# Affinities with the centroids as weights on four column groups, maxima of four heads at once before the first exponentials, and two batches' statistics ahead of step 0

## The chip, the cores and the metric

The kernel runs on 1 core of one Trainium2 chip. The metric is the device time of one execution in microseconds (us). The kernel before was run 5 times: median 2185.6 us, from 2184.82 to 2187.02.

## What is computed

Two layers over x, 8 batches of 512 tokens with 256 features; all data are float32. Cut to what matters here:

```python
xn = layernorm(x)
# layer 0: attention, 16 heads of 16 features, softmax over all 512 keys
out0 = softmax(q @ k.T) @ v
# layer 0: mixture of 8 experts, each token goes to the nearest centroid
aff = xn @ centroids.T                      # 4096 tokens x 8
assign = argmax(aff, axis=1)
alpha = sigmoid(aff[assign])
h = layernorm(xn, ln_g[e], ln_b[e]); ye = xn + relu(h @ w1[e].T + b1[e]) @ w2[e].T + b2[e]
x = x + out0 + alpha * ye + (1 - alpha) * xn
# layer 1: causal attention, a convolution over its output, causal attention again, and a low-rank feed-forward
```

## The kernel before, in words

**Tiles and stages.** Tokens of a batch lie on 128 partitions in 4 chunks (`NC`). A batch is normalised twice: `first_norm` (L546) makes xn on ACT (L236), which feeds attention and affinities, and on POOL the input h of the experts (L553), which is normalised with the second row of `rs`. `first_features` (L567) transposes xn on PE into xT (`to_features`, L245): the first half of the features is copied out of PSUM by DVE (L247), the second by ACT (L249). `affinities` (L573) multiplies a batch's xT, as weights of 128 columns, with the 8 centroids as the moving operand (L577: 4 chunks x 2 halves of the features; every float32 matmul shows as two records, so 16) and DVE copies the 128x32 result (L584).

**Attention of layer 0** is 32 jobs (8 batches x 4 groups of four heads) of 8 steps each. The loop in `run` goes through steps t = 0 to 268. Step t does two things: `scores` (L323) computes the score blocks of one block of 128 queries for two heads, and DVE reduces each to its row maximum (L340); `exps` (L372), 12 steps later (`LEAD`), computes scores again with the maxima as a shift, and ACT makes the exponentials (L399). `attend` (L412) multiplies with the values every second step, `l0_done` adds the result to acc (L843 to L851). So the first 12 steps have maxima only, and the last 12 have exponentials only. In each step four matmuls on four row groups of 32 rows, two of maxima and two of exponentials, are issued together; in the first 12 steps only two are. The maxima have three PSUM banks (`mx`). When a job's maxima are there, `shift` (step 8 of the next job plus 1) transposes them (L353), DVE copies them (mT, L358) and SP writes them into a row of q by four DMAs (L360).

**What fills the steps.** After the matmuls of a step, `Work.fill` issues pieces: those with due times (projections L272, values L282, shifts), and a stream. The stream begins with the list `FIRST`, one entry per step, whose letters stand for statistics of a batch (s, L219), closing a group's norms (c, L224 to L231: group a is batch 0, b batches 1 to 3, e batches 4 to 7), xn and h (n), transposes (f) and affinities (a). FIRST has 11 entries. Then `routing` takes the maximum over the experts and the one-hot matrix (L620 to L634), counts with two matmuls (L640, L641), makes ranks (L643 to L653) and places (L657 to L680), and scatters the 32 pieces of h into DRAM by POOL, one per step (L693). After the scatter the stream loads the first expert's weights (L708, POOL) and its tokens (hs, L715, SP), waits 5 steps, and computes 23 blocks of 256 tokens (L724, L746, L757 to L776), 2.05 units of cost per step. Then `second_norm` (L462 gathers, L477 residual, L219 statistics, L236 norm) handles the first four batches, one piece each third step.

**Order.** Every engine runs its instructions in the order in which the program issues them; PSUM banks are handed round in rings (`banks_first` until the routing, three for maxima and five for the rest; then `banks_alone`).

```python
for at, call in ((t, Job.scores), (t - lead, Job.exps)):
```

Of the kernel before, what the change touches and what calls it, by code (L numbers as in the profile page):

```python
# [9 lines left out]
F32 = mybir.dt.float32  # L10
# [3 lines left out]
ALU = mybir.AluOpType  # L14
# [5 lines left out]
P = 128  # L20
# [3 lines left out]
NC = S // P  # L24
# [3 lines left out]
PH = 32  # L28
NE = 8
# [23 lines left out]


FIRST = (
    "s1 s2", "s3 c1 n1 a0", "n2 f1 s4", "n3 f2 a1 s5", "f3 a2 s6", "s7 c2 n4 a3", "n5 f4", "n6 f5 a4", "n7 f6 a5",
    "f7 a6", "a7",
)


# [77 lines left out]
def block_kernel(ctx: ExitStack, tc: tile.TileContext, x, a0_wqk, a0_bqk, a0_wv, a0_bv, cent, experts,  # L138
                 a1_wqk, a1_bqk, a1_wv, a1_bv, conv_w, conv_b, out_w, out_b, u1, v1, f_b1, u2, v2, f_b2, out):
    nc = tc.nc  # L140
# [43 lines left out]
    def share_banks(**kinds):  # L184

        rings.update({k: list(v) for k, v in kinds.items()})

    def bank(kind="mm"):
        rings[kind].append(rings[kind].pop(0))
        return rings[kind][-1]  # L190


    def banks_first():
        share_banks(mx=banks[:3], mm=banks[3:])

    def banks_alone():
        share_banks(mx=banks[:3], sc=banks[3:6], av=banks[6:7], mm=banks[7:])
# [4 lines left out]
    class Norms:  # L202
# [4 lines left out]
        def __init__(self, pool, bs, nm, twice):  # L207
            self.bs, self.nm, self.twice = bs, nm, twice
            n = len(bs) * NC
            self.mv = pool.tile([P, n, 2], F32, name=f"mv{nm}", bufs=1)  # L210
            self.rs = pool.tile([P, 2 if twice else 1, n], F32, name=f"rs{nm}", bufs=1)
            self.rs1 = pool.tile([P, n], F32, name=f"rs1{nm}", bufs=1) if twice else None
            self.nm_t = pool.tile([P, n], F32, name=f"nm{nm}", bufs=1)

        def stats(self, i):
# [6 lines left out]
        def close(self):  # L222
            rs = self.rs
            nc.vector.tensor_scalar(rs[:, 0, :], self.mv[:, :, 1], EPS, None, ALU.add)  # L224
            if self.twice:
                nc.vector.tensor_scalar(rs[:, 1, :], self.mv[:, :, 1], 1.0 + EPS, EPS * EPS, ALU.mult, ALU.add)
            nc.scalar.activation(rs, rs, AF.Sqrt)
            nc.vector.reciprocal(rs, rs)
            if self.twice:
                nc.vector.tensor_scalar(self.rs1, rs[:, 0, :], 1.0, None, ALU.add)  # L230
            nc.vector.scalar_tensor_tensor(self.nm_t, self.mv[:, :, 0], -1.0, rs[:, 0, :], ALU.mult, ALU.mult)  # L231

# [5 lines left out]
                    scale=self.rs[:, 0, n : n + 1],  # L238
                )

    def to_features(src, dst, off, k, nm):

        ps = bank()
        for c in range(NC):
            nc.tensor.transpose(ps[:, c * P : (c + 1) * P], src[:, c, k * P : (k + 1) * P], ident)  # L245
        if k == 0:
            nc.vector.tensor_copy(dst[:, k, off : off + S], ps)  # L247
        else:
            nc.scalar.copy(dst[:, k, off : off + S], ps)  # L249
# [170 lines left out]
    def run(jobs, work_of, layer, per_step, most):  # L420
        steps, lead, av_at = STEPS[layer], LEAD[layer], AV_AT[layer]
        last = max(av_at)

        def attend(t):
            for i, blocks in av_at.items():
                j, r = divmod(t - lead - i, steps)
                if r == 0 and 0 <= j < len(jobs):
                    for kc in blocks:
                        jobs[j].attend(kc, kc == 0, i == last and kc == blocks[-1])
                    if i == last:  # L430
                        jobs[j].done(jobs[j], t)

        work_of.first()
        for t in range(steps * len(jobs) + lead + last - steps + 1):
            work_of.t = t
            mm, after = [], []
            for at, call in ((t, Job.scores), (t - lead, Job.exps)):
                j, i = divmod(at, steps)
                if 0 <= j < len(jobs):
                    m, a = call(jobs[j], i)  # L440
                    mm.append(m)
                    after.append(a)
            for together in zip(*mm):
# [79 lines left out]
    with ExitStack() as l0:  # L523
# [7 lines left out]
        nc.scalar.dma_start(out=wv0, in_=a0_wv)  # L531
        bv0 = w0.tile([P, D], F32, name="bv0")
        nc.scalar.dma_start(out=bv0, in_=a0_bv)
        cent_sb = w0.tile([P, 2, NE], F32, name="cent_sb")
        nc.scalar.dma_start(out=cent_sb, in_=cent)

        later = ExitStack()
        pre = later.enter_context(tc.tile_pool(name="pre", bufs=1))
# [7 lines left out]
        def first_norm(norms, i):  # L546
            b = norms.bs[i]
            xn = work.tile([P, NC, D], F32, tag="o", name=f"xn{b}")
            norms.norm(i, xn)
            h = pre.tile([P, NC, D], F32, tag="h0", name=f"h0_{b}", bufs=NB)  # L550
            for c in range(NC):
                n = i * NC + c
                nc.gpsimd.tensor_scalar(  # L553
                    h[:, c, :], acc[b][:, c, :], norms.mv[:, n, 0:1], norms.rs[:, 1, n : n + 1],
                    ALU.subtract, ALU.mult,
                )
                firsts0[b, c] = norms, n
            h0.append(h)
            return xn
# [7 lines left out]
        def first_features(b, xn):  # L567
            t = big.tile([P, 2, S], F32, tag="xT", name=f"xT{b}")
            for k in range(2):
                to_features(xn, t, 0, k, f"a{b}")  # L570
            xT.append(t)

        def affinities(b):  # L573
            ps = bank()
            for c in range(NC):
                for k in range(2):
                    nc.tensor.matmul(  # L577
                        ps[:, c * NE : (c + 1) * NE],
                        lhsT=xT[b][:, k, c * P : (c + 1) * P],
                        rhs=cent_sb[:, k, :],  # L580
                        start=(k == 0),
                        stop=(k == 1),
                    )
            nc.vector.tensor_copy(  # L584
                aff[:, b * NC : (b + 1) * NC, :].rearrange("p c e -> p (c e)"), ps[:, : NC * NE]
            )

        def pt(shape, name, tag=None, bufs=1):
# [192 lines left out]

        def stream():

            norms = [first_norms] + [Norms(pre, bs, nm, True) for bs, nm in (((1, 2, 3), "b"), ((4, 5, 6, 7), "e"))]
            of = {b: (n, i) for n in norms for i, b in enumerate(n.bs)}
            xns = {}

            def stats(b):
                of[b][0].stats(of[b][1])

            def norm(b):
                xns[b] = first_norm(*of[b])

            def features(b):
                first_features(b, xns.pop(b))

            def close(i):
                norms[i].close()

            do = {"s": stats, "c": close, "n": norm, "f": features, "a": affinities}  # L800
            for t, pieces in enumerate(FIRST):
                for p in pieces.split():
                    do[p[0]](int(p[1]))
                if t == 1:
                    for n in range(NBLK):
                        nc.sync.dma_start(out=hs_z[n], in_=zeros)
                yield At(t + 1)
            banks_alone()
            yield from routing()
            later.close()  # L810
            moe = later.enter_context(tc.tile_pool(name="moe", bufs=2, reuse_waits="tile"))
            load_ffn()
            nc.sync.dma_start(out=ob_sb, in_=out_b)
            fb2_sb = work.tile([P, D], F32, tag="og", name="fb2_sb")
            nc.sync.dma_start(out=fb2_sb, in_=f_b2)
            nc.gpsimd.tensor_tensor(ob_sb, ob_sb, fb2_sb, ALU.add)
            nxt = Block(moe, 0)
            yield At(todo.t + 5)
            banks_experts()
            nxt.features()  # L820
            yield 0.5
            for n in range(NBLK):
                blk = nxt
                for f2 in range(NFC // 2):
                    blk.hidden(f2)
                    yield 1.75
                    if f2 == 0 and n + 1 < NBLK:
                        nxt = Block(moe, n + 1)
                if n + 1 < NBLK:
                    nxt.features()  # L830
                    yield 0.5
                for j in range(TB // P):
                    blk.output(j)
                    yield 3.5
            banks_alone()
            yield from second_norm(range(NB - N_LATE), "c", lambda n: At(todo.t + n))
# [47 lines left out]
            todo.add(t0 + STEPS[0] + 1, t0 + STEPS[0] + 1, 0.2, job.shift)  # L884

        banks_first()
        first_norms = Norms(pre, (0,), "a", True)
        first_norms.stats(0)
        first_norms.close()
        first_features(0, first_norm(first_norms, 0))  # L890
        todo.stream = stream()
        run(jobs, todo, 0, MOE_PER_STEP, 99)
        later.close()
# [323 lines left out]
```

## Time and profile before

| what | us |
|---|---|
| median of 5 runs | 2185.6 |
| the profiled execution, its own time | 2185.78 |
| its span, first to last instruction | 2184.0 |
| PE busy | 2075.6 (95%) |
| DVE busy | 1236.1 (57%) |
| ACT busy | 863.4 (40%) |
| POOL busy | 195.6 (9%) |
| mean granted clock of PE | 0.953 |

The page gives shares of the whole span. The work of one stage is read from the windows (busy time of each engine and the clock that was granted to PE, 1.00 being full speed, in a stretch of the span), from the groups of instructions (count, busy us, mean ns of one, idle time before them and what ended it), and from the timeline of an engine (start, duration, line, operation, count, idle time before it and its releaser). Times are counted from the first instruction.

### The profile page before, as it was taken

The numbers are of one execution on the slowest core, as the hardware profiler recorded it, in microseconds if no ns is written. First come the engines' busy times: TensorE is split into PE (matmuls) and PEld (weight loads), VectorE is DVE, ScalarE is ACT, GpSimd is POOL, SyncE is SP. The second block draws the span as 40 slices with busy tenths as digits, with TensorE's granted clock in tenths as the row PEclk, the third lists the DMA queues.
The fourth block names the chain that finished last, engine by engine and source line by source line (L and its number), as shares of the span: only waits on it lengthen the run. The fifth ranks groups of instructions, "written<-read, shape, count | busy, mean of one in ns | idle before, by whom it ended". The sixth has DMA issues, their size and how long they took to land.

```text
span 2184.0 us, 35488 instructions
## 1 busy us (share of the span) xinstructions
PE 2075.6 (95%) x13664; PEld 1050.1 (48%) x13664; DVE 1236.1 (57%) x3569; ACT 863.4 (40%) x1674; POOL 195.6 (9%) x222
## 2 busy tenths in 40 slices
PE   7997999999999999996798999999999999999998
PEld 4522555555555555542133455554554555554554
DVE  5465454555555554555322566676666666666662
ACT  2243333333333333334353244444444444444443
POOL 4355000000000000003320000000000000000000
PEclk7599999999999999996699799999999999999999
DMA  5013212221221212201100000000000000000000
GB/s 205 1 42 126 78 61 102 93 102 66 88 102 52 102 62 101 93 16 51 58 0 1 1 2 2 2 2 11 2 12 2 12 2 12 2 12 2 12 2 20
DMA packets 37064, 93.53 MB, mean 43 GB/s; under 512 B 5792, under 2 KB 27936, under 8 KB 33952
## 3 DMA queue, kind: packets, MB, share of 16 engines
q0 software_dynamic: 6384, 59.78, 7.4%
q1 hardware_dynamic: 29792, 30.56, 4.3%
q8 instruction: 107, 1.75, 0.3%
q10 hardware_dynamic: 720, 0.93, 0.1%
q14 instruction: 61, 0.50, 0.1%
HBM read 70.03 MB, written 20.45 MB: 41 GB/s over the span
## 4 chain that ended last, share of the span: by engine, by line
PE 80%; DVE 5%; issue 3%; ACT 1%; POOL 1%; another core or an unknown queue 0%; DMA 0%; DVEq 0%; POOLq 0%; ACTq 0%
PE bank L323 26%; PE bank L412 12%; PE bank L746 8%; PE bank L767 8%; PE bank L272 4%; PE bank L1023 4%; PE bank L390 4%; PE bank L372 3%; PE bank L282 2%; PE bank L1041 2%; PE bank L927 1%; PE bank L1075 1%; PE bank L940 1%; DVE jk L343 1%; PE bank L245 1%
## 5 line engine op out<-in xcount | busy, mean ns | idle before, releaser
L399 ACT ACTIVATE e<-bank 128x512 f32<-128x512 f32 (+1 forms) x1280 | 640.3, 552 | 968.8 <-PE bank L372 494.5
L323 PE MATMUL bank<-k,q 32*128 32x512 f32 (+3 forms) x3072 | 777.4, 538 | 30.0 <-DVE m L340 25.2
L372 PE MATMUL bank<-q,k 32*128 32x512 f32 (+3 forms) x3072 | 706.2, 538 | 12.8 <-DMA q<-mT 11.0
L343 DVE CUSTOM_DVE_ANT_0 jk<-bank,cmask 128x512 bf16<-128x512 f32 (+3 forms) x1024 | 502.9, 491 | 241.7 <-PE bank L323 162.7
L323 PEld LDWEIGHTS bank<-k,q 32*128 32x128 f32 x3072 | 303.9, 187 | 394.0 <-issue 167.3
L340 DVE TENSOR_REDUCE m<-bank 128x1 f32<-128x512 f32 x512 | 329.3, 685 | 165.1 <-PE bank L372 122.2
L412 PE MATMUL bank<-e,v 128*32 128x512 f32 (+3 forms) x3072 | 324.0, 509 | 0.7 <-ACT e L399 0.7
L372 PEld LDWEIGHTS bank<-q,k 32*128 32x128 f32 x3072 | 272.6, 187 | 36.7 <-issue 23.9
L746 PE MATMUL bank<-hsT,w 128*128 128x256 f32 x736 | 182.0, 393 | 0.7 <-ACT e L399 0.7
L746 PEld LDWEIGHTS bank<-hsT,w 128*128 128x128 f32 x736 | 135.4, 192 | 70.8 <-issue 53.3
L767 PE MATMUL bank<-w,hT 128*128 128x256 f32 x736 | 169.0, 383 | 0.0
L767 PEld LDWEIGHTS bank<-w,hT 128*128 128x128 f32 x736 | 136.1, 190 | 35.6 <-issue 19.0
L412 PEld LDWEIGHTS bank<-e,v 128*32 128x32 f32 x3072 | 68.0, 109 | 145.4 <-issue 138.3
L390 PE MATMUL bank<-mask_t,ident_bf 128*128 128x128 bf16 (+1 forms) x768 | 124.1, 244 | 0.0
L390 PEld LDWEIGHTS <-ident_bf 128*128 128x128 bf16 x768 | 43.6, 97 | 157.7 <-issue 142.5
L759 DVE TENSOR_SCALAR hT<-bank,w 128x256 f32<-128x256 f32 x92 | 44.5, 484 | 114.0 <-ACT hT L757 114.0
L1023 PE MATMUL bank<-ctxT,cw_sb 128*128 128x256 f32 x384 | 90.0, 383 | 2.1 <-DVE q L262 1.8
L343 DVE DVE_READ_ACCUMULATOR2_ANT m<- 128x1 f32 x1024 | 85.0, 83 | 0.4
L851 POOL TENSOR_TENSOR acc<-acc,og 128x256 f32<-128x256 f32 x32 | 23.2, 725 | 626.2 <-DVE og L847 626.2
L264 ACT ACTIVATE k<-bank,bqk,rows 128x512 f32<-128x512 f32 x64 | 46.3, 774 | 81.8 <-PE bank L272 71.7
L776 DVE TENSOR_TENSOR f<-bank,w 128x256 f32<-128x256 f32 x46 | 19.6, 425 | 102.1 <-PE bank L767 102.1
L1023 PEld LDWEIGHTS bank<-ctxT,cw_sb 128*128 128x128 f32 x384 | 70.1, 189 | 13.3 <-DVE q L262 3.2
(180 smaller groups left out, 1477.1 us busy)
## 6 DMA issues: line engine op xcount, KB each, us to landing
q<-mT SPq DMA_DIRECT2D x384, 2.0 KB
hs_d<-zeros SPq DMA_DIRECT2D x23, 256.0 KB
hs<-hs_d SPq DMA_DIRECT2D x23, 256.0 KB
fs_d<-f SPq DMA_DIRECT2D x23, 256.0 KB
acc<-in_x SPq DMA_DIRECT2D x8, 512.0 KB
out<-acc SPq DMA_DIRECT2D x8, 512.0 KB
cw_sb<-in_conv_w SPq DMA_DIRECT2D x1, 768.0 KB
wqk<-in_a_wqk ACTq DMA_DIRECT2D x1, 512.0 KB
```

The costliest lines, as they stand in the source:

```text
L264: nc.scalar.activation(dst, ps, AF.Identity, bias=bias[:, half : half + 1], scale=rows[:, half : half + 1])
L272: nc.tensor.matmul(ps, lhsT=w[:, k, col : col + P], rhs=src[:, k, :], start=(k == 0), stop=(k == 1))
L323: lambda h=h, qc=qc, at=at, nk=nk: nc.tensor.matmul(heads[h % 2][:, at : at + nk], lhsT=self.q[h * PH : (h + 1) * PH, qc * P : (qc + 1) * ...
L340: nc.vector.tensor_reduce(self.m[:, qc, h, :], src, AX.X, ALU.max, negate=True)
L343: nc.vector.tensor_tensor_reduce(out=junk[:, :nk], in0=src, in1=cmask[:, S - nk :], scale=1.0, scalar=-3e38, op0=ALU.add, op1=ALU.max, acc ...
L372: lambda h=h, kc=kc, at=at, lo=lo: nc.tensor.matmul(heads[h % 2][:, at : at + S - lo], lhsT=self.k[h * PH : (h + 1) * PH, kc * P : (kc + 1 ...
L390: nc.tensor.matmul(heads[h][:, : len(blocks) * P], lhsT=ident_bf, rhs=mask_t[:, : len(blocks) * P], start=False, stop=True,)
L399: nc.scalar.activation(e[:, h, :], heads[h][:, :n], AF.Exp, scale=self.scale)
L412: nc.tensor.matmul(self.av[h * PH : (h + 1) * PH, lo:], lhsT=self.v[:, kc, 4 * self.g + h, :], rhs=es[h // 2][:, h % 2, :], start=first, s ...
L746: nc.tensor.matmul(ps[:, i * TB : (i + 1) * TB], lhsT=w[:, O_W1 + k * FF + fc * P : O_W1 + k * FF + (fc + 1) * P], rhs=self.hsT[:, k, :], ...
L767: nc.tensor.matmul(ps[:, 0:D], lhsT=self.hT[:, fc, j * P : (j + 1) * P], rhs=w[:, O_W2 + fc * D : O_W2 + (fc + 1) * D], start=(fc == 0), s ...
L1023: nc.tensor.matmul(ps[:, :w], lhsT=cw_sb[:, k, tap, c * P : (c + 1) * P], rhs=ctxT[b % 2][:, k, tap + lo : tap + lo + w], start=(k == 0 an ...
```

## The change

- `cent_sb` is padded with zeros from 8 to 32 columns (a memset on DVE, and the DMA into the first 8). `affinities` loads the centroids as weights and streams xT; the four chunks go to four column groups of 32. The 128x128 result (expert by token) is copied by ACT (affT), transposed on PE, and DVE copies the 32 wanted columns into aff.
- In layer 0, steps below 12 do the maxima of two steps in each even step and none in odd ones, with four PSUM banks; the bank rings change at step 12.
- FIRST has 8 entries instead of 11; the statistics of batches 1 and 2 are issued ahead of step 0. Routing is issued from step 8 on instead of step 11, and so is all that follows it in the stream.
- Both halves of xT are copied by ACT.
- POOL's h is a multiplication and an addition instead of a subtraction and a multiplication; DVE makes the extra operand nm2 at each close.

```diff
-    "s1 s2", "s3 c1 n1 a0", "n2 f1 s4", "n3 f2 a1 s5", "f3 a2 s6", "s7 c2 n4 a3", "n5 f4", "n6 f5 a4", "n7 f6 a5",
-    "f7 a6", "a7",
+    "s3 c1 n1 a0", "n2 f1 s4 s5", "n3 f2 a1 s6 s7 c2", "f3 a2 n4", "f4 a3 n5", "f5 a4 n6", "f6 a5 n7",
+    "f7 a6 a7",
...
-        share_banks(mx=banks[:3], mm=banks[3:])
+        share_banks(mx=banks[:4], mm=banks[4:])
...
+                nc.vector.scalar_tensor_tensor(self.nm2, self.mv[:, :, 0], -1.0, rs[:, 1, :], ALU.mult, ALU.mult)
...
-        if k == 0:
+        if k == 0 and eng is None:
...
+            if layer == 0 and t == lead:
+                banks_alone()
+            if t >= lead or layer == 1:
+                maxima = (t,)
+            else:
+                maxima = (t, t + 1) if t % 2 == 0 else ()
-            for at, call in ((t, Job.scores), (t - lead, Job.exps)):
+            for at, call in [(i, Job.scores) for i in maxima] + [(t - lead, Job.exps)]:
...
-        cent_sb = w0.tile([P, 2, NE], F32, name="cent_sb")
-        nc.scalar.dma_start(out=cent_sb, in_=cent)
+        cent_sb = w0.tile([P, 2, PH], F32, name="cent_sb")
+        nc.vector.memset(cent_sb, 0.0)
+        nc.scalar.dma_start(out=cent_sb[:, :, :NE], in_=cent)
...
-                    h[:, c, :], acc[b][:, c, :], norms.mv[:, n, 0:1], norms.rs[:, 1, n : n + 1],
-                    ALU.subtract, ALU.mult,
+                    h[:, c, :], acc[b][:, c, :], norms.rs[:, 1, n : n + 1], norms.nm2[:, n : n + 1],
+                    ALU.mult, ALU.add,
...
-            for c in range(NC):
-                for k in range(2):
+            for k in range(2):
+                for c in range(NC):
                     nc.tensor.matmul(
-                        ps[:, c * NE : (c + 1) * NE],
-                        lhsT=xT[b][:, k, c * P : (c + 1) * P],
-                        rhs=cent_sb[:, k, :],
+                        ps[c * PH : (c + 1) * PH, 0:P],
+                        lhsT=cent_sb[:, k, :],
+                        rhs=xT[b][:, k, c * P : (c + 1) * P],
...
+            affT = pre.tile([P, P], F32, tag="affT", name=f"affT{b}", bufs=2)
+            nc.scalar.copy(affT, ps[:, 0:P])
+            ps = bank()
+            nc.tensor.transpose(ps[:, 0:P], affT, ident)
             nc.vector.tensor_copy(
-                aff[:, b * NC : (b + 1) * NC, :].rearrange("p c e -> p (c e)"), ps[:, : NC * NE]
+                aff[:, b * NC : (b + 1) * NC, :], ps[:, 0:P].rearrange("p (c e) -> p c e", e=PH)[:, :, :NE]
             )
...
-            banks_alone()
             yield from routing()
...
-        first_norms.stats(0)
-        first_norms.close()
-        first_features(0, first_norm(first_norms, 0))
+        norms[0].stats(0)
+        norms[0].close()
+        first_features(0, first_norm(norms[0], 0))
+        for i in range(2):
+            norms[1].stats(i)
```

More of the change, by code (lines that the diff above doesn't have):

```diff
@@ L212, in __init__ @@
             self.rs1 = pool.tile([P, n], F32, name=f"rs1{nm}", bufs=1) if twice else None
+            self.nm2 = pool.tile([P, n], F32, name=f"nn{nm}", bufs=1) if twice else None
             self.nm_t = pool.tile([P, n], F32, name=f"nm{nm}", bufs=1)
@@ L239, in norm, with to_features @@
                 )
-    def to_features(src, dst, off, k, nm):
+    def to_features(src, dst, off, k, nm, eng=None):
         ps = bank()
@@ L569, in first_features @@
             for k in range(2):
-                to_features(xn, t, 0, k, f"a{b}")
+                to_features(xn, t, 0, k, f"a{b}", "s")
             xT.append(t)
@@ L782, in stream @@
         def stream():
-            norms = [first_norms] + [Norms(pre, bs, nm, True) for bs, nm in (((1, 2, 3), "b"), ((4, 5, 6, 7), "e"))]
             of = {b: (n, i) for n in norms for i, b in enumerate(n.bs)}
@@ L886, in block_kernel @@
         banks_first()
-        first_norms = Norms(pre, (0,), "a", True)
-        first_norms.stats(0)
-        first_norms.close()
-        first_features(0, first_norm(first_norms, 0))
+        norms = [Norms(pre, bs, nm, True) for bs, nm in (((0,), "a"), ((1, 2, 3), "b"), ((4, 5, 6, 7), "e"))]
+        norms[0].stats(0)
[3 more added lines that the diff above has]
+            norms[1].stats(i)
         todo.stream = stream()
```

## The prediction, made before the changed kernel was run

> **What bounds the kernel now.** PE is busy for 95% of the span, but that is a mean over stages, and the change edits only the first one. So I read the busy time and granted clock by window, then the groups and timelines of 0 to 225 us, and last the end of layer 0. Columns of the window line: stretch, length, busy us of PE, PEld, DVE, ACT, POOL, granted clock, DMA share, GB/s.
>
> ```profile
> 57.00:89.00 32.00, 31.84 (x119) 22.87 (x117) 9.88 (x19) 9.89 (x20) 18.70 (x16) 0.50 0.00 1
> ```
>
> Here PE has no gap, at half clock, and the others are mostly idle: PE is the bound. In order of time (start, us):
>
> ```profile
> 62.07 1.97 PE L245 MATMUL bank<-ident,xn 128*128 128x128 f32 x8
> 63.83 3.42 PE L577 MATMUL bank<-cent_sb,xT 128*128 128x8 f32 x16
> 67.18 2.08 PE L323 MATMUL bank<-k,q 32*128 32x512 f32 x4
> 69.19 1.97 PE L245 MATMUL bank<-ident,xn 128*128 128x128 f32 x8
> ```
>
> A step takes 7.1 us: transposes, one affinity of 16 matmuls that stream 8 columns each after a 128-column weight load (3.42 for almost no work), and one pair of maxima (2.08).
>
> The routing at the end of this stage releases the scatter of 32 pieces on POOL, and that releases the experts. First and last scatter, then the first expert weights (POOL); then what PE does meanwhile:
>
> ```profile
> 113.92 1.21 POOL L693 DMA_INDIRECT hs_d<-h,pos_i  x1 [38.22 <-issue]
> ...
> 205.28 1.02 POOL L693 DMA_INDIRECT hs_d<-h,pos_i  x1 [1.09 <-DMA hs_d<-h,pos_i]
> 206.35 0.55 POOL L565 TENSOR_SCALAR acc<-acc,rs1e,nme 128x256 f32<-128x256 f32 x1
> 206.88 0.71 POOL L816 TENSOR_TENSOR ob_sb<-ob_sb,fb_sb 128x256 f32<-128x256 f32 x1
> 208.58 1.00 POOL L708 DMA_INDIRECT w<-in_experts,wrow_i  x1 [0.99 <-DMA hs_d<-h,pos_i]
> ```
>
> ```profile
> 203.91 2.05 PE L323 MATMUL bank<-k,q 32*128 32x512 f32 x4
> 216.92 2.08 PE L372 MATMUL bank<-q,k 32*128 32x512 f32 x4 [10.96 <-DMA q<-mT]
> 218.93 1.11 PE L724 MATMUL bank<-ident,hs 128*128 128x128 f32 x4
> 220.73 8.09 PE L746 MATMUL bank<-hsT,w 128*128 128x256 f32 x24 [0.69 <-ACT e L399]
> ```
>
> Each scatter waits for the one before (91.4 us for 31 intervals, 2.95 each), and PE has run out of steps at 206: from here to 221 the scatter, not PE, sets the time. **So the gain is read at the first scatter (113.92), not from PE's saved work.** From 221 to 975 PE is busy 98 to 100%; nothing there is edited.
>
> **The change, worked out as a chain to the first scatter.** (Rows on the left are of before; L numbers are its own.)
>
> 1. Start. The memset of cent_sb and the new nm2 are two small DVE operations, some 0.1 each (small ones start 0.08 to 0.1 apart): +0.2. The cent_sb DMA now waits for that memset at about 6.6 (3.0 before), and ACT's table load (1.28) and first square root stand behind it: load done at about 8.5, square root due at 9.2, so hidden by 0.7. It lands in 32-byte pieces, but its first reader comes at 21. xT's first half by ACT (0.59) instead of DVE (0.69): nothing. First maxima at 20.3 (20.11).
> 2. Statistics of batches 1 and 2 (8 x 0.53 = 4.2) go to DVE's idle 9.9 to 17.0: hidden if x has landed; at 340 to 400 GB/s batch 2 (2.5 MB in all with the weights) lands by 9.5. Four maxima on four row groups: the later rows have four such matmuls in 1.1 (0.70 + 0.59, overlapped), so 21.4. Four reductions 2.5, statistics of batch 3 2.1, close 1.25: 27.3. Before, the first xn of batch 1 started at 31.31: 4.0 gained.
> 3. xn 2.07, then the first affT copy, for which PE waits, having nothing else in its order (128x128 on ACT: between 0.23 of a 128x32 and 0.59 of a 128x512 copy, I take 0.3): 29.75. Affinity transpose 0.25, transposes of xn 1.97: 32.0.
> 4. PE: maxima 2.1, xn2 2.0, affinity 1, ACT's copy and its wait 0.4, transpose 0.25: 37.75. DVE: statistics 4 and 5 after aff0 (30.2), four reductions, aff1 at 37.8, statistics 6 and 7 4.2, close 1.3: 43.5. Before, 56.5.
> 5. From 45.7 on ACT paces batches 4 to 7: xn 2.07, PE's transposes after its last piece 1.0, xT copy 0.6, affT 0.3, handovers 0.2: 4.2 each (7.1 before), to 62.5. The six maxima of steps 4 and 6 and most affinities lie beside xn. Last two affinities: 64.5.
> 6. Four maxima 2.1, reductions 2.5 after the first: 68. Maximum to one-hot took 94.33 to 100.19; 3.0 of that was a wait for ACT, which stood in k (1.45) and the table load (1.28); now ACT is idle: 2.9, so 71. The two count matmuls 2.0, cum to rank 3.35, four reductions 2.5, q 1.5 (its projection, 5.65, is ready by 79), place and pos_i 3.65: 84.1. POOL answers in 0.9: **first scatter at 85.0, 28.9 earlier.**
>
> The affinity itself: 8 matmuls of 512 columns on four column groups (L412) take 1.06 at full clock, so 16 of 128 columns 0.53, at half clock 1.06; upper end 3.42, the old price, if loads still rule. I take 1.06, as L412 has this tiling; on the path lie some 0.5 of it. POOL's h falls from 1.22 to 0.55 each (the row of L565, mult and add); POOL has 30 us to spare, so nothing.
>
> The clock: I keep 0.50 from 30 us on, as 57 to 89 shows that gapless PE alone didn't raise it. If it is 1.0, chain items of PE halve, some 8 us less.
>
> [...]
>
> **Scatter to experts.** 36 steps of PE (92 us for 37 before) and 91.4 of scatter still run side by side. Before, PE then waited for q<-mT, queued on SP behind hs, which waits for the last scatter. The experts now start in step 49, not 52; its exps need no new q, so PE waits for hs itself, ahead of q<-mT on SP. Worth between 0 and 3 (the 2.08 of L372 and part of the queue): 1.5.
>
> **What is given back.** Everything from routing on runs three steps earlier in a loop of 269 steps, so the experts end at step 243, not 246, and three more steps follow them. The last steps have exponentials only, at half clock:
>
> ```profile
> 1045.43 2.08 PE L372 MATMUL bank<-q,k 32*128 32x512 f32 x6
> 1048.19 2.07 PE L372 MATMUL bank<-q,k 32*128 32x512 f32 x2 [0.67 <-ACT e L399]
> 1050.18 1.94 PE L412 MATMUL bank<-e,v 128*32 128x512 f32 x8
> 1052.05 2.08 PE L372 MATMUL bank<-q,k 32*128 32x512 f32 x6
> ```
>
> Five took 1045.4 to 1061.4, 3.2 each: three more, +9.6 (5.8 at the 1.93 of 1014 to 1018). And the last residual and statistics group (L477, L219; 1016.6) now has maxima of three steps before it on DVE, 3 x 1.2 less the mT copy: +3.4 (0 if hidden). Together +13.0, bounds 5.8 to 14.
>
> **Sum**, against the profiled execution of 2185.8 (span 2184.0, 1.8 around it; the runs' median is 2185.6): 2185.8 - 28.9 - 1.5 + 13.0 = **2168.4**.
>
> **Rivals.**
> - *The stall at 989 goes.* In the chain that ended last there is
>
> ```profile
> 989.14 7.15 another core or an unknown queue
> ```
>
> with DVE and ACT both idle amid POOL's gathers. Nothing in the program asks for it; with other instructions beside the gathers it may not recur: 2168.4 - 7.2 = 2161.
> - *The scatter paces longer.* Its first intervals were 3.4, not 2.95, while the clock was half. If 3.45 held for 31 intervals: + 15.5 = 2183.9, no change. Against: it fell to 2.72 soon after.
> - *The affinities don't get cheaper.* 2.36 more each, 8 times: + 18.9 = 2187.3, no change. Against: L412.
> - *Slower: the new round trip PE, ACT, PE.* If each affT copy stood behind ACT's xn (2.07) and two copies (1.1), PE would wait 3.2 each, 8 times: + 25.6 = 2194. It decides from 2.15 us each (17.2 / 8). For: the first one does wait so. Against: each later copy is issued after the xT copies and ahead of the next xn, when PE has just finished.
>
> **How the numbers follow.** Chances: forecast 0.64 (own range 2160 to 2178, from the bounds of clock, tail and experts), stall gone 0.20, scatter 0.05, affinities 0.04, slower 0.07. Faster by over 0.2% (4.4 us, about what a measurement of this kernel can tell) is 0.64 + 0.20 = 0.84; within 0.09; slower 0.07. The range goes from 2152 (stall gone and PE at full clock) to 2182, which takes in the bounds of the tail and half of the scatter case.
>
> **What would show it.** First xn of batch 1 at 27 (step 2); close of batches 4 to 7 at 43.5; L577's successor at 0.5 to 1.1 per 16; first scatter at 85; last one 91 later; first L746 at about 190; five exponential-only steps become eight at 3.2. Wrong would be: PE idle for 2 us or more before each affinity transpose, a scatter pace above 3, or experts that start late though the scatter ended early.

## The result: no difference, and the profile after

The changed kernel's runs have a median of 2186.1 us (44 runs, 2163.9 to 2201.5), the kernel before beside them 2184.5 us (86 runs). The ratio of changed to before is 0.9994, with a 95% interval from 0.9982 to 1.0005: no change, where 2168.4 was forecast. (The ratio leaves out runs over 1.5% above the fastest of their kernel, so it lies below the ratio of the two medians.) The profiled execution took 2180.98 us (span 2179.2, mean granted clock 0.962). In the lines of after, L325, L374, L414 and L761 are the L323, L372, L412 and L746 of before, L588 is the affinity, L598 the transpose behind it, L708 the scatter and L342 the maxima's reduction.

The start went as forecast. The window 57 to 89 of the kernel after, with the columns shown before:

```profile
57.00:89.00 32.00, 21.39 (x106) 8.68 (x104) 22.00 (x62) 9.73 (x20) 3.34 (x4) 0.74 0.02 8
```

PE is busy for 21 of 32 us in place of 31.8, and at 0.74 of full clock in place of 0.50. In order of time, on PE:

```profile
52.73 0.64 PE L588 MATMUL bank<-xT,cent_sb 128*32 128x128 f32 x16
53.81 0.33 PE L598 MATMUL bank<-ident,affT 128*128 128x128 f32 x1 [0.44 <-ACT affT L596]
54.07 1.14 PE L325 MATMUL bank<-k,q 32*128 32x512 f32 x8
```

An affinity costs 0.64 here, at full clock (1.00), and 1.08 where e1 (the same kernel profiled again) ran it at half clock; before it cost 1.85 at full clock (from 42.0 on, at 1.00) and 3.42 at half (from 46.3 and from 63.8 on, at 0.50). Its round trip through ACT costs 0.39 to 0.44 of waiting, but for the first, which waits 7.61 for a copy that stands behind the first xn on ACT. First and last scatter (POOL), then the experts' start (PE):

```profile
83.70 1.21 POOL L708 DMA_INDIRECT hs_d<-h,pos_i  x1 [31.91 <-issue]
...
175.15 1.02 POOL L708 DMA_INDIRECT hs_d<-h,pos_i  x1 [1.10 <-DMA hs_d<-h,pos_i]
```

```profile
180.48 1.09 PE L739 MATMUL bank<-ident,hs 128*128 128x128 f32 x4 [5.35 <-DMA hs<-hs_d]
187.85 4.37 PE L761 MATMUL bank<-hsT,w 128*128 128x256 f32 x10 [6.28 <-DVE hsT L744]
```

The first scatter is 30.2 us earlier, the first expert matmul 32.9. The end of the span is 4.8 us earlier. So 28 us were lost behind the experts' start. The lengths of all stages, in us (landmarks read from the timelines of POOL and PE; the experts' stretch goes from the start of their first matmul to the end of the last; e1, e2, e5 and e15 are experiments below):

| stage | before | after | e2: before again | e1: after again | e5: experts in step 52 | e15 |
|---|---|---|---|---|---|---|
| to the first scatter | 113.9 | 83.7 | 112.5 | 87.0 | 89.1 | 89.2 |
| to the last scatter | 91.4 | 91.4 | 93.9 | 94.6 | 92.5 | 93.0 |
| to the first expert matmul | 15.4 | 12.7 | 15.6 | 12.9 | 15.6 | 17.2 |
| the experts' stretch | 754.6 | 767.9 | 754.7 | 765.7 | 754.8 | 752.1 |
| to the feed-forward (end of layer 0) | 88.5 | 88.9 | 68.3 | 83.2 | 80.6 | 71.7 |
| to the first maxima of layer 1 | 131.2 | 132.1 | 130.9 | 130.3 | 131.6 | 131.2 |
| to the last output projection ahead of the final pair (L1075, L1090 of after) | 941.5 | 942.3 | 937.4 | 943.8 | 937.4 | 941.3 |
| to the end | 47.5 | 60.2 | 55.4 | 55.3 | 55.6 | 53.1 |

Before and after as first profiled differ, from top to bottom and before rounding, by -30.2, +0.1, -2.7, **+13.3**, +0.4, +0.8, +0.8 and **+12.7**: the sum is -4.8. Two rows take the gain back. They are of different kinds, as the columns of e1 and e2 show: the experts' stretch repeats, the last row does not.

**The experts' stretch.** Its window, of before and then of after:

```profile
220.73:975.28 754.55, 744.69 (x4100) 399.75 (x4100) 395.42 (x715) 270.53 (x502) 38.27 (x46) 1.00 0.22 79
```

```profile
187.85:955.75 767.90, 750.60 (x4092) 403.44 (x4096) 394.83 (x712) 269.71 (x502) 37.45 (x45) 1.00 0.22 79
```

The same instructions, but for a few at the edges, at the same full clock: PE is idle for 17.3 us in place of 9.9 (length less busy time) and 5.9 busier. What PE waited for in it (us in total, times, longest), of before and of after:

```profile
PE bank L323 <- DVE m L340: 9.9, 12, 1.2
```

```profile
PE bank L325 <- DVE m L342: 17.3, 24, 1.2
```

Twice as many waits for the maxima. One of them in detail, in e1, on PE and then on DVE:

```profile
246.32 0.59 PE L325 MATMUL bank<-k,q 32*128 32x512 f32 x2
246.34 0.59 PE L374 MATMUL bank<-q,k 32*128 32x512 f32 x2
248.11 1.29 PE L325 MATMUL bank<-k,q 32*128 32x512 f32 x3 [1.18 <-DVE m L342]
248.72 0.70 PE L374 MATMUL bank<-q,k 32*128 32x512 f32 x2
```

```profile
245.93 0.72 DVE L856 STREAM_TRANSPOSE avt<-bank 128x512 f32<-128x512 f32 x1 [0.60 <-PE bank L414]
...
247.03 0.42 DVE L860 TENSOR_TENSOR og<-avt,rec 128x256 f32<-128x256 f32 x1
247.38 1.28 DVE L342 TENSOR_REDUCE m<-bank 128x1 f32<-128x512 f32 x2
```

PE ended a step's scores at 246.9. That step, of odd number, got no piece of the stream, and the values' matmuls (L414, 1.07), which come in even steps, had been the step before; so the next step's maxima are due at once. While the experts run, the maxima have two PSUM banks (`banks_experts`; the three named ahead of the prediction hold outside the steps of the experts), both filled by the step before, and DVE, held up by a finished job's output (L856 to L860), empties the first only at 248.1. PE loses 1.18 us waiting, and some 0.6 more because the maxima now start alone and the exponentials' scores follow instead of running beside them: 248.11 to 249.84, 1.73 for what takes 1.13 (245.79 to 246.93). That second part stands in the profile as busy time. By the totals, 12 more waits cost 7.4 idle and 5.9 busy. Nearly all of the busy part lies in the two score matmuls. Their busy time together, of before and then of after (columns here: PE, PEld, DVE):

```profile
220.73:975.28 754.55, 236.45 (x1548) 69.97 (x1548) 18.36 (x24) 1.00 0.22 79
```

```profile
187.85:955.75 767.90, 241.77 (x1544) 72.47 (x1544) 18.35 (x24) 1.00 0.22 79
```

That is 5.3 of the 5.9.

**The tail.** The exponential-only steps that had run at half clock in before (2.08 for four L372 records, at 0.50), in after:

```profile
1036.56 1.07 PE L414 MATMUL bank<-e,v 128*32 128x512 f32 x8
1037.55 1.13 PE L374 MATMUL bank<-q,k 32*128 32x512 f32 x6
```

They ran at full clock (1.00 from 1036.5 to 1038.7). The stall among POOL's gathers, 7.15 us before, is half as long in the chain that ended last:

```profile
969.34 3.47 another core or an unknown queue
```

Both hid that three more steps were there. In before's second profile (e2) this stage took 68.3, not 88.5.

### The profile page after: what moved, and what is told of

Same layout as the page of the kernel before. It is cut to its first block, busy times and chain, and to the rows that moved or that the text cites. A ratio compares the mean times of both kernels' runs of the same rounds, so it can differ in the third digit from the quotient of the medians.

```text
span 2179.2 us, 35533 instructions
## 1 busy us (share of the span) xinstructions
PE 2044.6 (94%) x13672; PEld 1029.0 (47%) x13672; DVE 1231.3 (57%) x3565; ACT 868.5 (40%) x1690; POOL 173.5 (8%) x222
## 4 chain that ended last, share of the span: by engine, by line
PE 83%; DVE 6%; issue 5%; DMA 4%; POOL 1%; ACT 1%; another core or an unknown queue 0%; ACTq 0%; POOLq 0%; DVEq 0%; SPq 0%
PE bank L325 27%; PE bank L414 12%; PE bank L761 8%; PE bank L782 8%; PE bank L274 5%; PE bank L392 4%; PE bank L1038 4%; DMA hs_d<-h,pos_i 4%; PE bank L374 3%; PE bank L284 2%; PE bank L1056 2%; PE bank L1090 1%; PE bank L247 1%; PE bank L942 1%; DVE m L342 1%
## 5 line engine op out<-in xcount | busy, mean ns | idle before, releaser
L325 PE MATMUL bank<-k,q 32*128 32x512 f32 (+3 forms) x3072 | 767.1, 537 | 37.2 <-DVE m L342 33.3
L374 PE MATMUL bank<-q,k 32*128 32x512 f32 (+3 forms) x3072 | 705.0, 536 | 1.7 <-ACT e L401 1.7
L325 PEld LDWEIGHTS bank<-k,q 32*128 32x128 f32 x3072 | 302.4, 187 | 403.7 <-issue 161.4
L342 DVE TENSOR_REDUCE m<-bank 128x1 f32<-128x512 f32 x512 | 329.1, 685 | 163.9 <-PE bank L374 124.5
L414 PE MATMUL bank<-e,v 128*32 128x512 f32 (+3 forms) x3072 | 323.3, 509 | 0.7 <-ACT e L401 0.7
L374 PEld LDWEIGHTS bank<-q,k 32*128 32x128 f32 x3072 | 274.3, 187 | 24.6 <-issue 15.0
L761 PE MATMUL bank<-hsT,w 128*128 128x256 f32 x736 | 183.5, 395 | 6.3 <-DVE hsT L744 6.3
L761 PEld LDWEIGHTS bank<-hsT,w 128*128 128x128 f32 x736 | 135.7, 193 | 77.2 <-issue 61.5
L414 PEld LDWEIGHTS bank<-e,v 128*32 128x32 f32 x3072 | 68.3, 110 | 137.1 <-issue 130.9
L266 ACT ACTIVATE k<-bank,bqk,rows 128x512 f32<-128x512 f32 x64 | 46.3, 773 | 87.4 <-PE bank L274 77.3
L772 ACT ACTIVATE hT<-bank,w 128x256 f32<-128x256 f32 x92 | 43.6, 474 | 91.1 <-PE bank L761 90.3
L1038 PEld LDWEIGHTS bank<-ctxT,cw_sb 128*128 128x128 f32 x384 | 70.1, 189 | 13.3 <-DVE q L264 3.2
```

Of the source, the lines that this page charges most:

```text
L266: nc.scalar.activation(dst, ps, AF.Identity, bias=bias[:, half : half + 1], scale=rows[:, half : half + 1])
L325: lambda h=h, qc=qc, at=at, nk=nk: nc.tensor.matmul(heads[h % 2][:, at : at + nk], lhsT=self.q[h * PH : (h + 1) * PH, qc * P : (qc + 1) * ...
L342: nc.vector.tensor_reduce(self.m[:, qc, h, :], src, AX.X, ALU.max, negate=True)
L374: lambda h=h, kc=kc, at=at, lo=lo: nc.tensor.matmul(heads[h % 2][:, at : at + S - lo], lhsT=self.k[h * PH : (h + 1) * PH, kc * P : (kc + 1 ...
L414: nc.tensor.matmul(self.av[h * PH : (h + 1) * PH, lo:], lhsT=self.v[:, kc, 4 * self.g + h, :], rhs=es[h // 2][:, h % 2, :], start=first, s ...
L761: nc.tensor.matmul(ps[:, i * TB : (i + 1) * TB], lhsT=w[:, O_W1 + k * FF + fc * P : O_W1 + k * FF + (fc + 1) * P], rhs=self.hsT[:, k, :], ...
```

## The experiments

Ratios are to runs of the kernel before on the same chip. e1 to e4 ran on one chip, e5 to e8, e9 to e12 and e13 to e15 on three others.

**e1 and e2: both kernels again, unedited.**

> The changed kernel, unedited, looked at again. Theory 1 (the gain is there, and the clock in the stretches where PE has only two row groups at work takes it back in some executions): first scatter at 83.7 and first expert matmul at 188 again, within 1 us; but the stretch from 2100 to the end, 79 us at a granted clock of 0.76 in the first look, comes out anywhere between 65 us (0.96, as in the kernel before) and 79, and the execution's time moves with it, 2166 to 2181. Rival (the loss is a fixed part of the new order): all landmarks and the end repeat within 2 us, 2179 to 2183.

> The kernel before, unedited, looked at again, for the same table of stages. Theory 1: its last 65 us are at full clock and the tail of layer 0 (975 to 1064, clock 0.66) is at half, or they swap; its time is 2185 with both as in the first look, up to 14 more if the last stretch falls to half clock as well, 8 to 10 less if the tail of layer 0 rises to 0.81. Rival: every stage repeats within 2 us.

e1: 2185.0 (12 runs, 2174.5 to 2198.9), ratio 1.0035 (1.0006 to 1.0064). e2: 2174.8 (12 runs, 2165.5 to 2186.7), 0.9996 (0.9969 to 1.0023). The first expert matmul and the experts' stretch repeated to 7 and 2 us; the tail of layer 0 and the last row of the table moved by 6 to 20 and by 5 to 8. The landmarks of e1's start, expected again within 1 us, came 3.3 (first scatter) and 6.6 later (first expert matmul). Theory 1 was right in that these stages vary with the clock within one kernel, and wrong in that they would be the whole loss: the stretch is fixed.

**e3: idle scores on the free row groups in both tails.**

```diff
+            if steps * len(jobs) <= t < steps * len(jobs) + lead:
+                m, a = jobs[-1].idle_scores(t % steps)
```

> The changed kernel, with work added that nothing uses: in the last 12 steps of each layer, which have exponentials only, the score matmuls of the other two row groups are issued beside them, into the PSUM banks of the maxima, and ACT reads two columns of each. Theory 1 (PE is granted half clock because only two of four row groups work): the clock from 2100 to the end stays at 0.95 or more in place of 0.76 and that stretch falls from 79 to 66 us; the tail of layer 0 runs at 0.85 or more; 2162 to 2168 in all, and the runs lie closer together than the 38 us of the changed kernel. Rival (the clock falls by chance or by what ran before it): clock and times as without the addition, plus 48 small reads of about 0.2 us on ACT, 0 to 5 us slower, 2181 to 2186.

2173.2 (12 runs, 2160.7 to 2181.7), 0.9976 (0.9949 to 1.0003), against 1.0035 of e1 on the same chip: between what theory 1 and its rival had expected. The end of layer 1 in windows, of after and then of e3:

```profile
2133.00:2160.00 27.00, 27.00 (x123) 11.15 (x126) 0.68 (x2) 8.36 (x18) 0.00 (x0) 0.52 0.00 1
```

```profile
2110.84:2150.00 39.16, 36.34 (x301) 18.06 (x300) 6.95 (x24) 17.13 (x57) 0.00 (x0) 1.00 0.04 15
```

In after PE has no gap in 27 us and is granted half clock; in e3, with all four row groups at work, full clock. That fits theory 1. But the last row stayed at 55.2 us (55.3 in e1). Up to the last scores e3 took 33.7 where e1 took 36.8; but from the final pair of projections to the end, where nothing was added, it took 13.3 at a clock of 0.50 where e1 took 9.8 at 0.88, and that took the gain back.

**e4, e5, e9: when the experts begin.** Between the first expert's loads and its first matmul the program waits 5 steps; here 7, 8 and 6.

```diff
-            yield At(todo.t + 5)
+            yield At(todo.t + 8)
```

> The changed kernel, with the wait between the first expert's loads and its first matmul raised from 5 to 7 steps. PE waits 6.28 us there for the tokens (hsT) now. If two more steps of attention fit into that wait: the first expert matmul stays at 188 within 1 us with less than 2 us of wait ahead of it, and everything behind comes 4.5 us earlier (two steps of 2.1 to 2.6). Rival (those steps need a q whose DMA is queued behind the tokens' on SP): PE waits as long, for q<-mT instead, as in the kernel before (10.96), and nothing is gained.

> The changed kernel, with the wait between the first expert's loads and its first matmul raised from 5 to 8 steps, so that the experts begin in step 52 of the loop again, as in the kernel before, and end in step 246. Theory (what is lost behind the scatter comes from the shift of three steps: it puts the expert pieces beside other attention pieces, so that PE waits for DVE's maxima 17.3 us in place of 9.8 between the first and last expert matmul, and it leaves three more steps with exponentials only): the experts' stretch falls from 766 to 755 us with about 9.8 us of those waits, the tail from the last expert matmul to the feed-forward falls by 8 or more at equal clock (83 in the last look, with 15 us of it lost to half clock), and the median is 2150 to 2160 on this chip, where the kernel before has 2174. Rival (the lengths of those stretches are set by the clock of each execution): they stay at 766 and 83, and the median at 2166 (two steps later) to 2185. Second rival (PE runs out of steps, waiting for q<-mT behind the tokens' DMA): first expert matmul at 196 to 200 in place of 194, and 4 us of the gain are gone.

> The changed kernel with a wait of 6 steps, so that the experts begin in step 50 of the loop and end in step 244. Attention multiplies with the values in every even step. Counted from the program's order, the odd steps between the first and last expert piece that get no piece at all are 11 with the experts in step 52 (12 waits for DVE's maxima were seen), 21 in steps 49 and 51 (24 and 22 seen), and 14 in step 50. Theory (odd steps without a piece make PE wait for DVE): 13 to 16 waits, 10 to 13 us of them, experts' stretch 756 to 760 us though the experts begin only one step later than in the changed kernel. Rival (the loss falls with every step by which the start comes nearer to 52): 18 to 23 waits, 15 us or more, stretch 763 to 768.

| kernel | first step of the experts | odd steps without a piece | waits for DVE | us | stretch | median | ratio |
|---|---|---|---|---|---|---|---|
| before | 52 | 11 | 12 | 9.9 | 754.6 | 2184.5 | 1 |
| after | 49 | 21 | 24 | 17.3 | 767.9 | 2186.1 | 0.9994 (0.9982 to 1.0005) |
| e9 | 50 | 14 | 14 | 11.3 | 757.6 | 2159.0 | 0.9905 (0.9877 to 0.9933) |
| e4 | 51 | 21 | 22 | 16.0 | 765.6 | 2166.5 | 0.9957 (0.9932 to 0.9983) |
| e5 | 52 | 11 | 12 | 9.9 | 754.8 | 2159.7 | 0.9896 (0.9867 to 0.9924) |
| e12 | 54 | 13 | 13 | 12.5 | 766.4 | 2154.7 | 0.9872 (0.9838 to 0.9905) |
| e13 (before, one step later) | 53 | 23 | 24 | 19.6 | 769.8 | 2208.8 | 1.0099 (1.0069 to 1.0128) |

The third column is counted from the program's order, without a chip, a shift's short transpose not counting as a piece: each step hands out pieces until its budget of 2.05 is used, so which steps stay empty follows from the step in which the experts begin. The waits go with that count and not with the distance to step 52: e9, one step from after, has 14, as its theory had it. Starts in an even step have 11 to 14, in an odd step 21 to 23. (e12's stretch has another cause, below.)

In e4 the wait ahead of the first expert matmul stayed (7.04 for hsT), but its two steps were done in time: the start was no later (192.8, e1 194.5). In e5 PE waits 6.2 for q<-mT instead, as the second rival had it, and the first matmul comes at 197.2. Yet the median falls by 1% of before. The tail tells the rest: e5's took 80.6, e1's 83.2, but by the 5 us windows below 0.97 of full clock (5 x (1 - clock), summed) e5 lost 20.4 of it and e1 15.4. Without that, 60.2 and 67.8: an estimate of 7.6 us for three steps. The other profiles without added matmuls, treated alike, put it higher: 67.8 to 72.6 with the experts in step 49 (after, e1, e14) and 54.5 to 61.5 in step 52 (before, e2, e5, e6, e7, e10), 12 us between the means.

**e13: the kernel before, one step later.**

> The kernel before, none of the change in it, with its wait ahead of the experts raised from 5 to 6 steps: they begin in step 53 in place of 52. By the count of the program's order the odd steps without a piece rise from 11 to 23. Theory (the parity of the experts' first step sets PE's waits for DVE, whatever precedes it): 22 to 26 waits, 16 to 19 us in place of 9.8, experts' stretch 764 to 768 in place of 755; one step fewer with exponentials only gives 2 to 3 back; 7 to 10 us slower than before. Rival (the longer stretch belongs to the changed kernel, through its banks or its earlier start): 12 waits and 755 again, 2 us faster.

```profile
226.23:995.99 769.76, 750.16 (x4092) 402.67 (x4096) 394.64 (x712) 270.39 (x502) 37.49 (x45) 1.00 0.22 80
```

The stretch grows by 15.2 in a kernel without any of the change, with 24 waits for 12, PE busy for 750.2 as in after (750.6). The kernel is 1% slower (some 22 us), more than expected: the first expert matmul, too, comes 4.3 to 5.5 later (226.2), behind a wait of 16.7 for q<-mT. This settles the stretch: neither the new affinities nor the banks of the first steps cause it, the first step of the experts does.

**e14 and e15: a third bank.**

```diff
-        share_banks(mx=banks[:2], sc=banks[4:6], av=banks[6:7], mm=banks[2:4] + banks[7:])
+        share_banks(mx=banks[:3], sc=banks[4:6], av=banks[6:7], mm=banks[3:4] + banks[7:])
```

> The changed kernel with its own start of the experts (step 49), but with three PSUM banks for the maxima in place of two while the experts run, the third taken from the five users of the common ring, which keeps two of three. Theory (PE waits for DVE because a step's maxima need both banks that the step before filled): with a third bank one of the two maxima of a step can always be issued, waits for DVE's maxima fall from 17.3 us to under 10 and the stretch from 767 to 752 to 760. Rival (DVE itself is behind, whatever the banks, or the ring that gave the bank is now short): waits of the same sum, for hT, hsT, f or the maxima; stretch 765 or longer.

> The changed kernel with the experts in step 52, idle score matmuls on free row groups in the last 12 steps of each layer (both as in e8) and three PSUM banks for the maxima while the experts run. Theory: if the third bank helps in e14, it takes most of the 9.9 us of waits that e8 still had: stretch 747 to 752, median 3 to 8 us under e8's ratio of 0.986 to before, at 0.983. Rival (the common ring with two banks makes PE wait elsewhere): 0.986 or higher.

e14's waits in the stretch:

```profile
PE bank L325 <- DVE m L342: 1.4, 4, 0.4
```

From 17.3 to 1.4: the wait was for a bank. The stretch fell to 759.1 (767.9), less than the waits did, since PE was busier still (756.8): the two score matmuls together took 250.2 (241.8 in after) at the same clock of 1.00, which would fit more of them running one after the other instead of side by side, as in the step of e1 above (1.73 for 1.13). Why the third bank does that wasn't followed up. 2179.0 (12 runs), 0.9966 (0.9939 to 0.9992). e15 (the changed kernel, experts in step 52, e8's idle scores, third bank) has the lowest ratio: 2150.8 (5 runs, 2150.1 to 2152.1), **0.984 (0.9812 to 0.9868)**, faster than both kernels. Its interval overlaps those of e8 and e12 and just touches that of e5, so what the third bank adds isn't shown.

**e6, e7, e10: parts of the change on the kernel before.** e6 has the new affinities and centroids alone, e7 the maxima of two steps at once, e10 both with the old list of 11 entries. All begin the experts in step 52.

> The kernel before, with the new affinities and the padded centroids alone; the list of first pieces, the maxima, the statistics and the start of the routing in step 11 are those of before. Theory: the 16 matmuls fall from 3.42 to 0.64 us, less the transpose and its wait (0.25 + 0.4), 2.1 each on a stretch that PE bounds: 17 us off the first scatter (112.5 to 96) and off the first expert matmul (222 to 206); the experts still begin in step 52, so nothing is given back behind them: median 2157 on this chip, 17 below before. Rival (the wait for ACT's copy costs what the matmuls save): first scatter later than 108, median above 2170.

> The kernel before, with the maxima of two steps taken together in each even step of the first 12 and four PSUM banks for them, alone. Theory (it matters for the granted clock and for PE's time beside the list of first pieces): in 20 to 115, where before lost 38 us to half clock, PE's maxima fall from 2.08 per step to about 1.1 and the clock rises above 0.67; first scatter 4 to 10 us earlier (103 to 108), median 2164 to 2170. Rival (DVE's four reductions in a row hold up the affinities' and features' copies queued behind them): first scatter at 112 or later, median 2174 or more.

> The kernel before with the new affinities and the maxima of two steps at once, but its own list of first pieces (11 entries, routing in step 11, both halves of the features copied as before, no statistics ahead of step 0). Theory (the two parts together make most of the start's gain, and the shorter list adds some): first scatter at 92 to 97 (89 with the whole change on the same experts' step, 99 and 103.5 with one part alone), first expert matmul at 200 to 205 with the experts in step 52, experts' stretch 755, median 2160 to 2167 on a chip where before has 2185. Rival (the shorter list is what the gain needs): first scatter at 99 or later, median 2170 or more.

| kernel | first scatter | first expert matmul | stretch | median (runs) | ratio |
|---|---|---|---|---|---|
| e6 | 103.5 | 211.5 | 758.3 | 2181.9 (12) | 0.9967 (0.9945 to 0.9988) |
| e7 | 99.2 | 207.2 | 753.8 | 2170.4 (7) | 0.9927 (0.9906 to 0.9948) |
| e10 | 98.0 | 205.4 | 756.4 | 2168.9 (11) | 0.9932 (0.9909 to 0.9956) |
| e5 (with the rest of the change) | 89.1 | 197.2 | 754.8 | 2159.7 (6) | 0.9896 (0.9867 to 0.9924) |

Each part gains. The affinities gave 9 us of the 17 expected: up to the first scatter PE's busy time fell by 32 (93.7 to 61.4), but its idle time rose by 23 (18.8 to 42.1). Of the new idle time 18 stand in two waits for affT (9.87 and 8.21), whose copy comes behind the next batch's xn on ACT. The maxima gave more than expected, 13, and the two together hardly more than the maxima alone, so that e10 lies between its theory and its rival. The rest of the change (the shorter list with the early statistics, the copies by ACT, POOL's h) brings the first scatter 9 earlier still, if the experts keep their step.

**e8, e11, e12: towards a faster version.** e8 is e5 with idle scores that nothing reads, each row group with a bank of its own: in half of the steps all four groups are at work, in the others three. e11 is e5 with the tokens loaded by POOL's queue and the memset made by POOL; e12 is e11 with 10 steps of wait and e8's idle scores.

```diff
-                nc.sync.dma_start(
+                nc.gpsimd.dma_start(
                     out=self.hs, in_=hs_d[n * TB : (n + 1) * TB, :].rearrange("(j p) d -> p j d", p=P)
```

> As the run with the experts in step 52 (e5), with idle score matmuls on the free row groups beside the exponentials of the last 12 steps of each layer, each row group into a PSUM bank of its own and read by nothing. Theory (PE is granted half clock when only two of its four row groups work): no half clock in these two stretches but where PE waits; 10 to 20 us less than e5 in executions that would have lost them, median 2143 to 2152, and runs within 15 us of each other. Rival (the added matmuls take PE's time, as they did with reads on ACT, where the last slice stayed at 55 us in spite of a clock of 0.87): median that of e5 within 4 us.

> The run with the experts in step 52 (e5), with two edits: the experts' tokens (hs) are loaded by POOL's queue in place of SP's, and the memset of the centroids is made by POOL in place of DVE. Theory: the four q<-mT DMAs no longer stand behind the tokens' load, which waits for the last scatter, so PE's wait of 6.2 us for q<-mT ahead of step 52 goes; but the tokens themselves land at about 192, so the first expert matmul comes 1 to 4 us earlier (193 to 196 in place of 197.2); the first square root comes back from 11.0 to 9.1, and with it the first scatter 0 to 2 us earlier. Median 1 to 6 us under e5's. [...]

> As the run before it (e11), with the wait raised from 8 to 10 steps (experts in step 54, 13 odd steps without a piece) and idle score matmuls on free row groups in the last 12 steps of each layer (as in e8). Theory: two more steps of attention (5 us) fill what is left of the wait for the tokens; two fewer steps with exponentials only: 3 to 8 us under e11, and the runs closer together. Rival (q of the next job is missing at step 53 or 54, or the last block's end becomes late for the residual and statistics behind it): no gain over e11 within 3 us.

e8: 2155.6 (4 runs), 0.986 (0.9835 to 0.9885), whose interval overlaps e5's: not told apart. Half clock was not gone, as the theory had it: up to the last scores of layer 1 the clock was 0.81. e11: 2170.7 (12 runs), 0.9941 (0.9919 to 0.9963), above e5, with intervals that just overlap. The wait for q<-mT went, and one of 11.6 for the tokens themselves took its place; inside the stretch PE waited twice more for them (5.6), and it grew to 765.0 (754.8 in e5). The theory was right about the wait for q<-mT and wrong about the start: the first expert matmul came at 200.4, not at 193 to 196. e12, with two steps more to fill the wait, had less of it (4.5) and came out 16 us under e11, where 3 to 8 were expected; its stretch is long for the same reason (4.8 of waits for the tokens).

## Why the prediction was wrong, point by point

- **Start to first scatter: right, in part by luck.** Close of batches 4 to 7 at 43 (43.5 forecast), first scatter 83.7 and in e1 87.0 (85.0). Errors inside it cancel: the first square root came at 10.99 and not at 9.2, so that step 1 was not hidden, and the first maxima came at 20.98 (20.3); the clock was 0.73 to 0.86 in the windows from 20 to 84 us (0.50 to 0.85 in e1), not 0.50; so the affinity cost 0.64, and where the clock was half, in e1, 1.08, as forecast (1.06); batches 4 to 7 followed each other by 3.75 to 5.0 (4.75 to 5.85 in e1), not 4.2.
- **Scatter to experts: right.** 187.9 and 194.5, forecast 190. The pace was 2.95 (91.4 for 31) in after and 3.05 in e1.
- **"From 221 to 975 PE is busy 98 to 100%; nothing there is edited": this step failed.** Its instructions are unedited, but it was moved by three steps against the attention steps, whose work alternates with the step's number. Forecast 0, measured +13.3, and +11.0 between e1 and e2. The prediction gave it no term and no reason beyond the unedited code. "Busy 98 to 100%" was true and misled: the 9.9 us of waits in it were a number that the order could change, and half of the loss shows as busy time. The view that would have warned is the waits of PE in that window, which names the releaser (DVE's maxima), beside the banks' shares in the code.
- **What is given back: right in kind, and of about the size, as far as the clock lets one say.** Forecast +13.0 (5.8 to 14). Profile against profile it was +0.4, because before's tail happened to hold a long stall (7.15) and ran at a clock of 0.66 (0.81 in after); e1 against e2 +14.9; at equal clock, by the estimates beside e5, +7.6 to +12.
- **Layer 1: not forecast at all.** It lost 12.7 in the last row in the first pair of profiles: 8.3 up to the last scores and 3.5 from the final pair of projections on, both with the clock (1.00 and 0.90 in before, 0.70 and 0.63 in after). Its code is the same, and e1 against e2 shows -0.1 there: the first profile of before had simply the shortest last row of all.
- **Rivals.** Neither the longer pace, nor dear affinities, nor the round trip (0.44 of wait, decisive from 2.15) came true; the stall at 989 halved, and e2 shows how far that stage moves by itself; the slower case named the wrong wait.

The sum with what was measured: first expert -30.4 (mean of after, e1, e3 and e14: 191.0, of before and e2: 221.4; the forecast had -28.9 - 1.5), stretch +12.8 (mean of after, e1 and e3: 767.4, of before and e2: 754.6), tail +7.6 to +12: -10 to -5. Measured: -1.3, from -3.9 to +1.1. Some 4 to 9 us stay open. They are of the size by which the clock moves layer 1 from one execution to the next (8.3 up to the last scores, above), but that the changed kernel falls on the bad side more often is not shown. Nor is why its runs spread over 38 us and e15's over 2.

## What to carry to other kernels

A stage that is not edited is not a constant when the change moves it: if its pieces are dealt out between steps that alternate, count from the program's order which steps they miss before and after the move, and look up which wait lives there. When an early stage gets faster, keep the later stages in the steps that they had, and give the steps won to whatever waits, as e5 did: the same change then gains 1% (e5), and 1.6% in e15, with a third bank and the idle scores beside it. One profile of each kernel can't price a stage whose clock varies: compare stages in two or three executions first.

## What the runs showed of the hardware

The granted clock fell to half while PE had no gap at all (27.00 of 27.00 us busy at 0.52), in a stretch where the scores used two row groups of 32 rows. How much that costs can be read where the same work ran at either clock: from the last output projection ahead of the final pair to the last scores of layer 1, in before and then in after:

```profile
2136.50:2165.16 28.66, 28.50 (x198) 13.12 (x197) 6.26 (x22) 14.45 (x30) 0.00 (x0) 1.00 0.06 20
```

```profile
2119.02:2155.97 36.95, 36.87 (x198) 16.36 (x197) 6.26 (x22) 14.55 (x30) 0.00 (x0) 0.70 0.04 15
```

Of the 13 profiles without idle scores, 11 ran this stretch at 0.70 to 0.72 and took 36.8 to 37.0 us; two (the first of before, and e6) ran it at 1.00 and 0.98 and took 28.7 and 29.0. With all four groups in half of the steps and three in the others the clock was 0.81 (e8), 0.95 (e12) and 0.90 (e15), and with all four always (e3) 1.00. These four profiles suggest that the number of rows at work matters; it isn't shown apart from the number of matmuls, and the two profiles at full clock show that two row groups alone don't decide it.

A shift by one step in one number of the program (e13) cost 1%, 22 us, more than the whole change was meant to gain (17).
